# Projections as four column tiles, a merged diagonal step and sums behind the values in an fp32 attention kernel

## Chip, cores and metric

One core of a Trainium2 chip. The time is that of one execution on the device in microseconds; each kernel was executed several times, in rounds beside the kernel before on the same chip. A ratio is the mean time of one kernel's fast runs over that of the other's fast runs of the same rounds, so it is not quite the ratio of the medians quoted beside it. e1 to e4 ran on one chip, e5 to e8 on a second and e9 to e11 on a third; over the rounds the median of the kernel before lay between 2330.8 and 2335.1 us, so differences of a few microseconds between kernels of different groups should not be read.

## The reference

```python
# x: (32, 256, 32, 32) fp32; 8 heads of 32 channels; S = 1024 positions
xn   = group_norm(x, groups=32)                     # groups of 8 channels
q    = q_w @ xn + q_b ;  k, v = split(kv_w @ xn + kv_b)
s    = q k^T / sqrt(32), strictly below the diagonal only (query > key)
out  = x + softmax(s) v                             # position 0 attends to nothing
```

## The kernel before

Everything is fp32, and each fp32 matmul runs as two passes (the trace has eight records for the four matmuls of one step's scores). A *row tile* is a matmul that uses 32 of the 128 rows of TensorE's array, a *column tile* one that uses 32 of its 128 columns; four of them stand side by side. Each way of dividing the array is a *mode* below. PSUM is the memory that TensorE writes to, in banks; a bank is *evacuated* when another engine has read the result out of it. One batch element ("batch" below) is two groups `g` of four heads; each group has two halves `hf` of 512 queries, and each half goes through its blocks `k` of 128 keys. A *step* is one (g, hf, k): 24 a batch. At each step TensorE computes the scores of four heads, ScalarE their exponentials, GpSimd zeroes the triangle of a diagonal block; two steps later (`LAG`) TensorE multiplies with the values, and VectorE adds the exponentials up. In between stand pieces of the next batches: twelve projections a batch, four sums over keys, and two small products for the statistics.

Projections, sums and statistics share **one PSUM bank** (`misc`, `bufs=1`), which the next user gets only when the one before has been evacuated.

```python
ps_s = tc.alloc_tile_pool(name="ps_s", bufs=3, space=PSUM)   # scores, 2 banks each
ps_o = tc.alloc_tile_pool(name="ps_o", bufs=1, space=PSUM)   # acc
ps_m = tc.alloc_tile_pool(name="ps_m", bufs=1, space=PSUM)   # the one bank
def misc(name):
    return ps_m.tile([P, HALF], F32, tag="misc", name=name)

def norm_rstd(b):                                   # statistics, second product
    pv = misc(f"pv_{b}")
    nc.tensor.matmul(pv[:, :NG], lhsT=avg, rhs=live.pop(("dev", b)), start=True, stop=True)
    rstd = small.tile([P, NG], F32, tag="rstd", name=f"rstd_{b}")
    nc.vector.tensor_scalar_add(rstd, pv[:, :NG], 1e-5)
    ...
def project_v(b, n):
    pp = misc(f"ppv_{b}_{n}")...
    # 2 x 2 matmuls of 128x128 by 256 columns
    nc.vector.tensor_add(live["v", b][...], pp, v_bias...)     # evacuated by VectorE
# project_qk: the same with 512 columns, evacuated by ScalarE

def scores(b, g, hf, k):                            # four row tiles (K = 32)
    for j in range(4):
        nc.tensor.matmul(pairs[j // 2][:, j % 2, c0:], lhsT=kk[rows_j, k * P : (k + 1) * P],
                         rhs=q[rows_j, hf * HALF + c0 : (hf + 1) * HALF], start=True, stop=True)
    ...
def values(b, g, hf, k):                            # four column tiles (M = 32)
    for j in range(4):
        nc.tensor.matmul(acc[HD * j : HD * (j + 1), c0:], lhsT=live["v", b][:, k, ...],
                         rhs=e[:, j, c0:], start=k == 0, stop=k == last, skip_group_check=True)
    if k:
        nc.vector.tensor_add(total[:, :, c0:], total[:, :, c0:], e[:, :, c0:])
...
for n, f in zip((4, 6, 10, 14, 16, 18), prepare(b + 2)):      # statistics, normalisation
    when(b * N + n, f)
for n, f in enumerate(projections(b + 1)):
    when(b * N + 2 * n + 1, f)
# main loop: scores(step i); whatever is planned at i; values(step i - LAG)
```

## Time and profile before

| | before |
|---|---|
| time, median | 2332.0 us (2330.8 to 2335.8) |
| busy TensorE / VectorE / ScalarE / GpSimd | 96% / 74% / 59% / 43% |
| period of one batch (start of one `pm` product to the next) | 70.7 us |
| granted TensorE clock (share of the full clock, mean) | 0.994 |

The period is the number to watch: 32 batches of it make up nearly all the time. The prediction below shows the lines of this profile and how they are read.

### The profile page before, as it was taken

Reading aid. Unit: us, or ns where it says so; the run is one execution under the profiler, and the core shown is the slowest. Engines: PE = TensorE matmul, PEld = TensorE weight load, DVE = VectorE, ACT = ScalarE, POOL = GpSimd, SP = SyncE. Lnnn points to the kernel's source line nnn. Section 1 sums busy time; section 2 is a strip of 40 time slices with the busy share of each in tenths; the row PEclk is TensorE's granted clock in tenths of the full one; section 3 lists DMA queues with packets and bytes.
Section 4 is the critical chain, followed back from the end, with each engine's and each line's share of the span. In section 5 each row is a group of like instructions: output and inputs, shape, how many; then the busy total and the mean of one; then the engine's idle time right before and its main releaser. Section 6 shows DMA issues by size and latency. Waiting matters only on the chain.

```text
span 2334.8 us, 37671 instructions
## 1 busy us (share of the span) xinstructions
PE 2243.6 (96%) x15502; PEld 824.2 (35%) x15502; DVE 1735.7 (74%) x1641; ACT 1386.2 (59%) x1921; POOL 1001.5 (43%) x817
## 2 busy tenths in 40 slices
PE   5999999999999999999999999999999999999995
PEld 2333333333333333333333333333333333333331
DVE  2477787877787777787777778777878777877777
ACT  0566666566566566566666665665665665665663
POOL 0234443534543434544434544344435345434346
PEclk9999999999999999999999999999999999999997
DMA  2001111011111011111011111111110111110001
GB/s 88 1 19 55 37 55 55 28 46 42 50 55 55 28 46 37 55 55 55 19 55 37 55 55 38 36 51 41 55 55 28 46 37 55 55 55 28 28 37 55
DMA packets 38033, 104.06 MB, mean 45 GB/s; under 512 B 4192, under 2 KB 5088, under 8 KB 37856
## 3 DMA queue, kind: packets, MB, share of 16 engines
q1 hardware_dynamic: 37856, 101.60, 11.8%
q8 instruction: 123, 2.02, 0.4%
q14 instruction: 54, 0.44, 0.1%
HBM read 34.47 MB, written 33.55 MB: 29 GB/s over the span
## 4 chain that ended last, share of the span: by engine, by line
PE 87%; DVE 8%; issue 2%; ACT 2%; POOL 1%; DMA 0%; SPq 0%; POOLq 0%; DVEq 0%
PE sT L215 27%; PE acc L243 23%; PE pp L176 21%; PE ppv L191 11%; PE pd L260 4%; DVE e L248 3%; DVE xn L163 2%; DVE v L196 1%; DVE den L268 1%; ACT num L252 1%; ACT q L180 1%; POOL e L225 1%; DVE rb L297 0%; PE pv L153 0%; PE pm L141 0%
## 5 line engine op out<-in xcount | busy, mean ns | idle before, releaser
L220 ACT ACTIVATE e<-sT 128x1024 f32<-128x1024 f32 (+3 forms) x1536 | 1148.4, 812 | 668.4 <-PE sT L215 456.3
L248 DVE TENSOR_TENSOR e<-e,e 128x2048 f32<-128x2048 f32 (+3 forms) x640 | 1130.9, 1767 | 221.2 <-PE acc L243 146.9
L225 POOL TENSOR_SCALAR_AFFINE_SELECT e<-e 128x512 f32<-128x512 f32 x512 | 733.3, 1441 | 1284.7 <-ACT e L220 1284.7
L215 PE MATMUL sT<-q,k 32*128 32x512 f32 (+3 forms) x6144 | 811.7, 534 | 0.5 <-ACT e L220 0.5
L243 PE MATMUL acc<-e,v 128*32 128x512 f32 (+3 forms) x6144 | 652.8, 497 | 20.0 <-ACT num L252 11.3
L176 PE MATMUL pp<-xn,wT 128*128 128x512 f32 x1024 | 513.3, 624 | 26.4 <-DVE den L268 20.7
L215 PEld LDWEIGHTS sT<-q,k 32*128 32x128 f32 x6144 | 288.0, 183 | 532.6 <-issue 277.6
L243 PEld LDWEIGHTS acc<-e,v 128*32 128x32 f32 x6144 | 134.9, 108 | 455.1 <-issue 366.3
L176 PEld LDWEIGHTS pp<-xn,wT 128*128 128x128 f32 x1024 | 175.0, 190 | 295.5 <-issue 205.7
L191 PE MATMUL ppv<-wT,xn 128*128 128x256 f32 x1024 | 255.2, 392 | 3.1 <-DVE v L196 2.3
L268 DVE TENSOR_TENSOR den<-den,pd 128x512 f32<-128x512 f32 x96 | 65.6, 684 | 220.2 <-PE pd L260 220.2
L298 POOL TENSOR_TENSOR rb<-rb,x 128x512 f32<-128x512 f32 x128 | 209.2, 1634 | 13.0 <-DVE rb L297 12.6
L191 PEld LDWEIGHTS ppv<-wT,xn 128*128 128x128 f32 x1024 | 184.1, 190 | 66.2 <-issue 33.8
L180 ACT ACTIVATE q<-pp,qk_bias 128x512 f32<-128x512 f32 x128 | 87.9, 687 | 137.4 <-PE pp L176 134.4
L196 DVE TENSOR_TENSOR v<-ppv,v_bias 128x512 f32<-128x512 f32 x128 | 88.3, 690 | 97.3 <-PE ppv L191 97.3
L260 PE MATMUL pd<-e,pick 128*32 128x512 f32 x1024 | 137.2, 608 | 1.2 <-DVE e L248 1.2
L297 DVE TENSOR_TENSOR rb<-num,rb 128x512 f32<-128x512 f32 x128 | 135.3, 1061 | 2.4 <-DMA rb<-rec 2.4
L180 ACT ACTIVATE k<-pp,qk_bias 128x512 f32<-128x512 f32 x128 | 88.1, 688 | 78.2 <-PE pp L176 75.2
L279 DVE RECIPROCAL rec<-den 128x128 f32<-128x128 f32 x128 | 118.7, 931 | 0.0
L252 ACT COPY num<-acc 128x512 f32<-128x512 f32 x128 | 74.2, 580 | 36.5 <-PE acc L243 36.5
L135 DVE BATCH_NORM_STATS2 st<-x 128x6 f32<-128x512 f32 x128 | 80.1, 668 | 4.7 <-DMA x<-in_x_dram 4.7
L163 DVE TENSOR_SCALAR xn<-x,mean,rstd 128x1024 f32<-128x1024 f32 x64 | 68.6, 1074 | 1.6 <-POOL rstd L156 1.6
(40 smaller groups left out, 254.6 us busy)
## 6 DMA issues: line engine op xcount, KB each, us to landing
x<-in_x_dram SPq DMA_DIRECT2D x32, 1024.0 KB, 5.8
rb<-rec SPq DMA_DIRECT2D x128, 256.0 KB, 2.5
out_dram<-rb SPq DMA_DIRECT2D x64, 512.0 KB, 3.0
wn<-in_L_conv_kv_w_dram SPq DMA_DIRECT2D x2, 256.0 KB, 3.4
wn<-in_L_conv_q_w_dram SPq DMA_DIRECT2D x1, 256.0 KB, 2.8
v_bias<-in_L_conv_kv_b_dram SPq DMA_DIRECT2D x1, 128.0 KB, 3.4
qk_bias<-in_L_conv_q_b_dram SPq DMA_DIRECT2D x1, 1.0 KB, 3.4
qk_bias<-in_L_conv_kv_b_dram SPq DMA_DIRECT2D x1, 1.0 KB, 3.1
```

Source lines behind the costliest of these rows:

```text
L176: nc.tensor.matmul(pp, lhsT=wT[:, cc, n * C + g * P : n * C + (g + 1) * P], rhs=live["xn", b][:, cc, cols], start=cc == 0, stop=cc == NG - 1,)
L180: nc.scalar.activation(live[key][:, cols], pp, AF.Identity, bias=qk_bias[:, n, g : g + 1], scale=(SCALE, 1.0)[n],)
L191: nc.tensor.matmul(pp[:, s, :], lhsT=live["xn", b][:, cc, (2 * n + s) * P : (2 * n + s + 1) * P], rhs=wT[:, cc, 2 * C : 3 * C], start=cc = ...
L215: nc.tensor.matmul(pairs[j // 2][:, j % 2, c0:], lhsT=kk[rows, k * P : (k + 1) * P], rhs=q[rows, hf * HALF + c0 : (hf + 1) * HALF], start= ...
L220: nc.scalar.activation(e[:, 2 * a : 2 * a + 2, c0:], pairs[a][:, :, c0:], AF.Exp)
L225: nc.gpsimd.affine_select(out=diagonal, in_=diagonal, pattern=[[0, 4], [1, P]], compare_op=ALU.is_gt, fill=0.0, base=0, channel_multiplier=-1,
L243: nc.tensor.matmul(acc[HD * j : HD * (j + 1), c0:], lhsT=live["v", b][:, k, h * HD : (h + 1) * HD], rhs=e[:, j, c0:], start=k == 0, stop=k ...
L248: nc.vector.tensor_add(total[:, :, c0:], total[:, :, c0:], e[:, :, c0:])
L260: nc.tensor.matmul(pd[HD * j : HD * (j + 1), :], lhsT=pick[:, n, :], rhs=total[:, j, :], start=True, stop=True, skip_group_check=True,)
L279: nc.vector.reciprocal(live["rec", b][:, cols], live["den", b][:, cols])
L297: nc.vector.tensor_mul(rb[:, g, cols], num[:, g, cols], rb[:, g, cols])
L298: nc.gpsimd.tensor_add(rb[:, g, cols], rb[:, g, cols], xt[:, g, cols])
```

## The change

The intent is to take mode changes away from TensorE. Scores use four row tiles, values and sums four column tiles, projections the full array, and each change between these costs time: 0.14 to 0.21 us, as the prediction works out from the trace. Projections are cut into four column tiles, so that they are in the values' mode; the 128-query diagonal block goes into the step of the 384-query one (20 steps a batch instead of 24); sums stand behind the values. The step plan is adapted to 20 steps.

```diff
+        def product(out, lhsT, rhs, start=True, stop=True):
+            for c in range(P // HD):
+                part = slice(HD * c, HD * (c + 1))
+                nc.tensor.matmul(out[part], lhsT=lhsT[:, part], rhs=rhs, start=start, stop=stop, ...)
 # norm_mean, norm_rstd, project_qk, project_v: nc.tensor.matmul(...) -> product(...)
+        def blocks(hf, k):
+            d = k - hf * BPH
+            own = slice(max(d, 0) * P, HALF)
+            if d == 1:
+                return [(k, own, own), (k + 2, slice(0, P), slice(HALF - P, HALF))]
+            return [(k, own, own)]
 # scores, values: a loop over blocks(hf, k) around the four matmuls (and the addition);
 # one exponential and one triangle select for both blocks
-        per = [... for k in range((hf + 1) * BPH)]
+        per = [... for k in range(hf * BPH + 3)]
-                for n, f in zip((4, 6, 10, 14, 16, 18), prepare(b + 2)):
+                for n, f in zip((3, 5, 8, 11, 14, 16), prepare(b + 2)):
-                    when(b * N + 2 * n + 1, f)                       # projections
+                    when(b * N + 1 + n * N // len(units), f)
-                    when(b * N + s + LAG + 2 + (s + LAG) % 2, ... sums)
+                    when(b * N + s + LAG + 1, ... sums, after)       # behind values
-                when(end + BPH + 5 + n, lambda b=b, n=n: finish(b, n))
+                when(end + BPH + 3 + n, lambda b=b, n=n: finish(b, n))
```

More of the change, by code (lines that the diff above doesn't have):

```diff
@@ L123, in misc @@
             return ps_m.tile([P, HALF], F32, tag="misc", name=name)
+        def product(out, lhsT, rhs, start=True, stop=True):
+            for c in range(P // HD):
+                part = slice(HD * c, HD * (c + 1))
+                nc.tensor.matmul(
+                    out[part], lhsT=lhsT[:, part], rhs=rhs, start=start, stop=stop, skip_group_check=True
+                )
         def load(b):
@@ L140, in norm_mean @@
             pm = misc(f"pm_{b}")
-            nc.tensor.matmul(pm[:, :NG], lhsT=avg, rhs=mv[:, :, 0], start=True, stop=True)
+            product(pm[:, :NG], avg, mv[:, :, 0])
             mean = small.tile([P, NG], F32, tag="mean", name=f"mean_{b}")
@@ L152, in norm_rstd @@
             pv = misc(f"pv_{b}")
-            nc.tensor.matmul(pv[:, :NG], lhsT=avg, rhs=live.pop(("dev", b)), start=True, stop=True)
+            product(pv[:, :NG], avg, live.pop(("dev", b)))
             rstd = small.tile([P, NG], F32, tag="rstd", name=f"rstd_{b}")
@@ L175, in project_qk @@
             for cc in range(NG):
-                nc.tensor.matmul(
-                    pp, lhsT=wT[:, cc, n * C + g * P : n * C + (g + 1) * P],
-                    rhs=live["xn", b][:, cc, cols], start=cc == 0, stop=cc == NG - 1,
+                product(
+                    pp, wT[:, cc, n * C + g * P : n * C + (g + 1) * P], live["xn", b][:, cc, cols],
+                    start=cc == 0, stop=cc == NG - 1,
                 )
@@ L190, in project_v @@
                 for cc in range(NG):
-                    nc.tensor.matmul(
-                        pp[:, s, :], lhsT=live["xn", b][:, cc, (2 * n + s) * P : (2 * n + s + 1) * P],
-                        rhs=wT[:, cc, 2 * C : 3 * C], start=cc == 0, stop=cc == NG - 1,
-                        skip_group_check=True,
+                    product(
+                        pp[:, s, :], live["xn", b][:, cc, (2 * n + s) * P : (2 * n + s + 1) * P],
+                        wT[:, cc, 2 * C : 3 * C], start=cc == 0, stop=cc == NG - 1,
                     )
@@ L204, in projections @@
             return units
+        def blocks(hf, k):
[4 more added lines that the diff above has]
+            return [(k, own, own)]
         def scores(b, g, hf, k):
             q, kk = live["q", b, g], live["k", b, g]
-            c0 = max(k * P - hf * HALF, 0)
+            d = k - hf * BPH
             tag = "e0" if k == 0 else "e"
@@ L212, in scores @@
             pairs = [ps_s.tile([P, 2, HALF], F32, tag="sT", name=f"sT_{b}_{g}_{hf}_{k}_{a}") for a in range(2)]
-            for j in range(4):
-                rows = slice(HD * j, HD * (j + 1))
-                nc.tensor.matmul(
-                    pairs[j // 2][:, j % 2, c0:], lhsT=kk[rows, k * P : (k + 1) * P],
-                    rhs=q[rows, hf * HALF + c0 : (hf + 1) * HALF], start=True, stop=True,
-                )
+            for kb, cols, of in blocks(hf, k):
+                for j in range(4):
+                    rows = slice(HD * j, HD * (j + 1))
+                    nc.tensor.matmul(
+                        pairs[j // 2][:, j % 2, cols], lhsT=kk[rows, kb * P : (kb + 1) * P],
+                        rhs=q[rows, hf * HALF + of.start : hf * HALF + of.stop],
+                        start=True, stop=True, skip_group_check=True,
+                    )
+            c0 = 2 * P if d == 2 else 0
             for a in range(2):
                 nc.scalar.activation(e[:, 2 * a : 2 * a + 2, c0:], pairs[a][:, :, c0:], AF.Exp)
-            if k * P >= hf * HALF:
-                diagonal = e[:, :, c0 : c0 + P]
+            if d >= 0:
+                n = 2 if d == 1 else 1
+                diagonal = e[:, :, c0 : c0 + n * P].rearrange("p j (n q) -> p j n q", q=P)
                 nc.gpsimd.affine_select(
-                    out=diagonal, in_=diagonal, pattern=[[0, 4], [1, P]],
+                    out=diagonal, in_=diagonal, pattern=[[0, 4], [0, n], [1, P]],
                     compare_op=ALU.is_gt, fill=0.0, base=0, channel_multiplier=-1,
@@ L233, in values @@
         def values(b, g, hf, k):
-            last = (hf + 1) * BPH - 1
-            c0 = max(k * P - hf * HALF, 0)
+            last = k == hf * BPH + 2
             e = live.pop(("e", b, g, hf, k))
@@ L240, in values @@
             acc, total = live["acc"], live["sum", b, g, hf]
-            for j in range(4):
-                h = 4 * g + j
-                nc.tensor.matmul(
-                    acc[HD * j : HD * (j + 1), c0:], lhsT=live["v", b][:, k, h * HD : (h + 1) * HD],
-                    rhs=e[:, j, c0:], start=k == 0, stop=k == last, skip_group_check=True,
-                )
-            if k:
-                nc.vector.tensor_add(total[:, :, c0:], total[:, :, c0:], e[:, :, c0:])
-            if k == last:
+            for kb, cols, of in blocks(hf, k):
+                for j in range(4):
+                    h = 4 * g + j
+                    nc.tensor.matmul(
+                        acc[HD * j : HD * (j + 1), of], lhsT=live["v", b][:, kb, h * HD : (h + 1) * HD],
+                        rhs=e[:, j, cols], start=k == 0, stop=last, skip_group_check=True,
+                    )
+                if k:
+                    nc.vector.tensor_add(total[:, :, of], total[:, :, of], e[:, :, cols])
+            if last:
                 if (g, hf) == (0, 0):
@@ L302, in finish, with when @@
                 nc.sync.dma_start(out=x_out[b, :, g, :], in_=rb[:, g, :])
-        per = [(g, hf, k) for g in range(NG) for hf in range(NH) for k in range((hf + 1) * BPH)]
+        per = [(g, hf, k) for g in range(NG) for hf in range(NH) for k in range(hf * BPH + 3)]
         steps = [(b, *s) for b in range(B) for s in per]
         N = len(per)
-        at = {}
-        def when(i, f):
-            at.setdefault(i, []).append(f)
+        at, after = {}, {}
+        def when(i, f, where=at):
+            where.setdefault(i, []).append(f)
         def prepare(b):
@@ L321, in unshifted @@
                 when(b * N, lambda b=b: load(b + 2))
-                for n, f in zip((4, 6, 10, 14, 16, 18), prepare(b + 2)):
+                for n, f in zip((3, 5, 8, 11, 14, 16), prepare(b + 2)):
                     when(b * N + n, f)
             if b + 1 < B:
-                for n, f in enumerate(projections(b + 1)):
-                    when(b * N + 2 * n + 1, f)
+                units = projections(b + 1)
+                for n, f in enumerate(units):
+                    when(b * N + 1 + n * N // len(units), f)
             for s, (g, hf, k) in enumerate(per):
-                if k == (hf + 1) * BPH - 1:
-                    when(b * N + s + LAG + 2 + (s + LAG) % 2, lambda b=b, g=g, hf=hf: sums(b, g, hf))
+                if k == hf * BPH + 2:
+                    when(b * N + s + LAG + 1, lambda b=b, g=g, hf=hf: sums(b, g, hf), after)
             end = (b + 1) * N + LAG + 2
@@ L351, in unshifted @@
                     values(*steps[i - LAG])
+                for f in after.get(i, ()):
+                    f()
             worst = const.tile([P, 1], F32, name="worst")
```

## The prediction

> **What bounds the kernel now.** I read first the engine line and the chain of waits on the page, then the groups by shape, then the timeline of TensorE and of VectorE over one steady batch (1000 to 1071 us), then TensorE's own waits and the start and end.
>
> ```profile
> PE 2243.6 (96%) x15502; PEld 824.2 (35%) x15502; DVE 1735.7 (74%) x1641; ACT 1386.2 (59%) x1921; POOL 1001.5 (43%) x817
> PE 87%; DVE 8%; issue 2%; ACT 2%; POOL 1%; DMA 0%; SPq 0%; POOLq 0%; DVEq 0%
> ```
>
> TensorE is busy 96% and is 87% of the chain that ends last. VectorE is second at 74%, and it is already 8% of that chain: it is where a faster TensorE will run into something. How TensorE spends its time shows only in its timeline (columns: start us, us, engine, line, operation, tiles, shape, count):
>
> ```profile
> 1000.23 1.31 PE L215 MATMUL sT<-q,k 32*128 32x512 f32 x8
> 1001.47 1.99 PE L176 MATMUL pp<-xn,wT 128*128 128x512 f32 x4
> 1003.38 1.06 PE L243 MATMUL acc<-e,v 128*32 128x512 f32 x8
> 1004.38 1.14 PE L215 MATMUL sT<-q,k 32*128 32x512 f32 x8
> 1005.45 1.07 PE L260 MATMUL pd<-e,pick 128*32 128x512 f32 x8
> 1006.33 1.04 PE L243 MATMUL acc<-e,v 128*32 128x512 f32 x8
> 1007.30 0.93 PE L215 MATMUL sT<-q,k 32*128 32x384 f32 x8
> ...
> 1021.19 0.42 PE L243 MATMUL acc<-e,v 128*32 128x128 f32 x8
> ...
> 1023.50 0.50 PE L215 MATMUL sT<-q,k 32*128 32x128 f32 x8
> 1023.94 1.99 PE L191 MATMUL ppv<-wT,xn 128*128 128x256 f32 x8
> ```
>
> Ends are modelled, so I take start to next start. A round of 512 columns takes 0.427 us whether it is one full 128x128 matmul or four narrow ones side by side (single matmuls of the trace: pp at 1002.002, 1002.431, 1002.861). What is above that is switching: scores (four row tiles) 1.07 us for two rounds (0.855), so 0.21 over; values (four column tiles) 0.99, so 0.14 over; sums followed by values, both column tiles, 0.88, so only 0.02 over; a projection 1.91 for four rounds (1.71), so 0.20 over. The overheads do not depend on the columns: scores 0.435 at 128, values 0.355 at 128.
>
> Summing these unstalled costs over one batch (two groups; scores 512, 384, 256, 128 and 5x512, 384, 256, 128): scores 20.6, values 18.7, twelve projections 23.0, four sums 3.5, two small statistics products 0.6, together 66.4 us. The measured period is 70.63 us (the same place at 1000.30 and 1070.93 in the chain of waits), so about 4.2 us a batch are waits inside scores for ScalarE's exponentials (a 384-column scores that takes 1.46 instead of 0.86, two 512 ones of 1.84 instead of 1.07) and for VectorE.
>
> **What the Trainium skill says.** "TensorEngine Tiling (Array Packing)", Key Properties: "Changing tiling mode (not just tile) drains the TensorE", and tiles work independently. The trace agrees: 0.02 us over between sums and values, 0.14 to 0.21 us at each change. "SBUF — State Buffer", in the section on its two sides: VectorE with two SBUF inputs and GpSimd lock each other out for a whole instruction. The trace agrees: a triangle select takes 0.63 us alone and 2.4 us beside an addition. "TensorE: Matmul & The Clock Gate", Part 1: after an idle window of some 3.4 us the clock is halved until a busy window. The trace is stricter (windows view: busy us of PE, PEld, DVE, ACT, POOL, then granted clock):
>
> ```profile
> 2288.90:2292.31 3.41, 2.04 (x20) 0.63 (x13) 3.41 (x4) 3.41 (x4) 3.41 (x3) 1.00 0.08 34
> 2292.31:2295.72 3.41, 3.41 (x20) 0.89 (x24) 3.31 (x3) 1.49 (x3) 3.35 (x3) 0.50 0.31 125
> ```
>
> A window with TensorE 60% busy (a gap of 1.37 us) is followed by one at half clock.
>
> **The change part by part.**
>
> Column tiles for projections: a projection becomes 16 (queries, keys) or 32 (values) narrow matmuls in the same number of rounds, four and eight. It now stands in the values' mode, so the change after it goes and the weights of the first round cost 0.03 instead of 0.11: 0.20 us each, 12 a batch, 2.4 us. I take it that four tiles that stream the same xn run as fast as four that stream different e. Issue is no limit: eight 128-column values with their loads need 0.22 us net. The small products: about 0.1 us each, 0.2 us.
>
> Merged diagonal: four steps of 128 columns a batch go. Each cost 0.435 for scores and 0.355 for values, of which 0.43 were rounds that stay; 0.36 us saved each, 1.4 us. ScalarE drops four pairs of exponentials (817 + 381 ns become 1024 ns: 0.17 us each of eight, 1.4 us), which lies off the path, but removes short steps in which it was late. VectorE has the same additions.
>
> Sums behind values: scores-sums-values becomes scores-values-sums, the same number of changes: 0.
>
> Sum on TensorE: 4.0 to 4.2 us a batch, 66.4 to 62.3 us. Going step by step through the 20 new steps, scores plus unit plus values against two exponentials (1.94 us a pair at 512 columns) and evacuations (0.69) and copies (0.58), ScalarE is never more than some 0.1 us late: of the 4.2 us of waits I keep 0.4. So far 62.7 us.
>
> What is given back is on VectorE. There is one bank for projections, sums and statistics; each user waits until the one before is evacuated. Now two such users stand at the same step 11: pv (the variance product) and then, at once, ppv of the third values projection. That one must wait until VectorE has read pv, and VectorE works in order. Before, there were some 1.75 us of TensorE work between, and it was just enough:
>
> ```profile
> 1013.00 0.15 DVE L143 COPY mean<-pm 128x2 f32<-128x2 f32 x1
> ...
> 1016.14 0.68 DVE L196 TENSOR_TENSOR v<-ppv,v_bias 128x512 f32<-128x512 f32 x1
> 1016.74 3.08 DVE L248 TENSOR_TENSOR e<-e,e 128x1536 f32<-128x1536 f32 x2
> 1019.73 1.12 DVE L297 TENSOR_TENSOR rb<-num,rb 128x512 f32<-128x512 f32 x1
> ...
> 1023.71 0.15 DVE L155 TENSOR_SCALAR rstd<-pv 128x2 f32<-128x2 f32 x1
> ```
>
> pv ran at 1022.19, its reader at 1023.71, the next user at 1023.94. In the new order VectorE has between mean and rstd: the 0.94 chain, two additions of 2048 (2.2 and 2.4), one v (0.6), the two of the merged block (1.85 and 0.72), one rb product (1.0): 9.7 us. TensorE has between pm and pv only values 0.99, step 9 3.36, step 10 2.07, scores 1.09 and pm 0.2: 7.7 us. VectorE enters late by 1.5 us (v 0.6, addition 2.2, reciprocal 0.87 after the first ppv, against 2.1 us of TensorE work). So 1.5 + 9.7 - 7.7, plus 0.2 of latency: TensorE stands still for 3.7 us, in every batch that has both (1 to 29; batch 0 has no earlier batch's reciprocals and products, 30 no statistics). The other waits on this bank (the copy of the sums before the next pp, pm before ppv) I put at 0.6 us.
>
> A gap of 3.7 us holds over 1.4 us of at least one 3.41 us window, so the clock halves. Until a full busy window has passed, 3.4 to 6 us of work run at half speed: 1.7 to 3 us lost in the unlucky phases, less if the gap covers the cold window. I take 2.0 us.
>
> Period: 62.7 + 0.6 + 3.7 + 2.0 = 69.0 us, 1.7 below 70.63. Over 29 batches 49 us; batches 0 and 30 without the stall 7 us each; the last batch without projections some 3 us, the start 1 us. 2331 - 67 = 2264 us.
>
> **The rivals.** (a) The stall is small or absent (VectorE less late, or the clock does not drop): the period is 63 to 65 us and the time 2120 to 2190 us. For it: VectorE idles over 16 us a batch today (waits on sums 220 us and on values 147 us in all). Against: those idle spans lie elsewhere in the batch; between mean and rstd there was only 0.45 us. (b) The stall is as I say or longer, and the clock stays low longer: the period is 70.5 to 72 us, 2300 to 2345 us. For it: selects on GpSimd delay additions (2.53 us instead of 2.28 at 1045.38). (c) Column tiles of projections are slower than a full array because four tiles read the same columns: nothing in the trace speaks for it; if each round took 10% more, 2 us a batch, about 65 us in all. (d) GpSimd's merged select (1024 elements) comes too late for the values: two steps later leaves some 5 us after the scores, the select needs some 3 under a lock; unlikely.
>
> **Range and chances.** The gain of 4.1 us and the removed ScalarE waits I hold for firm within 1 us a batch; stall and clock together may be 3 to 8 us. That gives 2190 to 2325 us eight times in ten. Over 2% faster means below 2284 us: 0.63. Slower by over 2% needs over 71.9 us a batch: 0.03. The rest, 0.34, within.
>
> **What would show it.** Right: pp at 1.71 us start to values, values after it with no change; merged scores 1.09; a TensorE wait of 3 to 4 us a batch at ppv, put down to rstd, or to a VectorE instruction; a granted clock of 0.93 to 0.97 in the mean. Wrong: no such wait, clock 1.00 (then rival a), or projections of over 1.8 us at full clock (rival c), or values waiting for the select (rival d).

## The result

| | before | after |
|---|---|---|
| time, median | 2332.0 us (2330.8 to 2335.8) | 2356.6 us (2354.0 to 2359.4) |
| ratio | | 1.0103 |
| period of a batch | 70.7 us | 71.68 us |
| granted clock | 0.994 | 0.951 |

The 95% interval of the ratio is 1.0083 to 1.0123: about 1% slower, within 2%, and outside the predicted range. Page of the changed kernel, engines and chain:

```profile
PE 2113.2 (90%) x22030; PEld 748.7 (32%) x22030; DVE 1732.8 (74%) x1641; ACT 1358.9 (58%) x1665; POOL 722.1 (31%) x689
PE 54%; DVE 40%; issue 5%; ACT 1%; DMA 0%; POOL 0%; SPq 0%; DVEq 0%; POOLq 0%; ACTq 0%
```

TensorE is busy 130 us less, and the time is longer all the same. VectorE does the same work as before, but its share of the chain went from 8% to 40%. TensorE's own waits say where (us in total, times, longest):

```profile
PE ppv L130 <- DVE rstd L164: 143.7, 30, 4.9
PE pd L282 <- DVE e L270: 23.2, 31, 2.6
```

Thirty waits of up to 4.9 us, one a batch, are at the place that the prediction named. TensorE's timeline there:

```profile
1014.00 0.82 PE L234 MATMUL sT<-q,k 32*128 32x256 f32 x8
1015.01 1.93 PE L130 MATMUL ppv<-wT,xn 128*32 128x256 f32 x32 [0.19 <-DVE mean L152]
1016.77 1.04 PE L265 MATMUL acc<-e,v 128*32 128x512 f32 x8
1017.74 1.14 PE L234 MATMUL sT<-q,k 32*128 32x512 f32 x8
1018.81 1.07 PE L265 MATMUL acc<-e,v 128*32 128x384 f32 x16
1019.81 1.31 PE L234 MATMUL sT<-q,k 32*128 32x384 f32 x16
1021.05 0.24 PE L130 MATMUL pv<-dev,avg 128*32 128x2 f32 x8
1026.17 3.64 PE L130 MATMUL ppv<-wT,xn 128*32 128x256 f32 x32 [4.87 <-DVE rstd L164]
1029.58 0.70 PE L265 MATMUL acc<-e,v 128*32 128x256 f32 x8
```

First, the gains are there: `ppv` to the values takes 1.76 us start to start (1015.01 to 1016.77), not 1.92, and the merged scores some 1.1 to 1.2. Then `pv` runs at 1021.05, and the `ppv` that follows it has to wait for VectorE's reading of `pv`, 4.87 us; and when it runs, it takes 3.41 us, twice its time. VectorE meanwhile:

```profile
1014.86 0.09 DVE L152 COPY mean<-pm 128x2 f32<-128x2 f32 x1
1015.00 0.16 DVE L155 TENSOR_TENSOR dev<-mv,mean 128x2 f32<-128x2 f32 x1
1015.19 0.97 DVE L156 TENSOR_TENSOR dev<-dev 128x2 f32<-128x2 f32 x1
1016.20 0.60 DVE L157 TENSOR_TENSOR dev<-dev,mv 128x2 f32<-128x2 f32 x1
1016.72 2.28 DVE L270 TENSOR_TENSOR e<-e,e 128x2048 f32<-128x2048 f32 x1
1018.92 0.68 DVE L204 TENSOR_TENSOR v<-ppv,v_bias 128x512 f32<-128x512 f32 x1
1019.52 5.93 DVE L270 TENSOR_TENSOR e<-e,e 128x2048 f32<-128x2048 f32 x3
1025.37 0.68 DVE L319 TENSOR_TENSOR rb<-num,rb 128x512 f32<-128x512 f32 x1
1025.97 0.14 DVE L164 TENSOR_SCALAR rstd<-pv 128x2 f32<-128x2 f32 x1
```

Between `mean` and `rstd` it is never idle for more than 0.1 us: 11.1 us of work in order, while TensorE had 8.3 us (1013.03 to 1021.29). The last view is the clock (stretches of one clock window each: length, then busy us of PE, PEld, DVE, ACT, POOL, then the granted clock):

```profile
1019.50:1022.90 3.40, 1.80 (x36) 1.39 (x28) 3.30 (x3) 3.26 (x4) 1.51 (x2) 1.00 0.28 103
1022.90:1026.30 3.40, 0.13 (x4) 0.13 (x8) 3.18 (x4) 0.03 (x1) 2.07 (x2) 0.50 0.01 2
1026.30:1029.75 3.45, 3.45 (x36) 1.61 (x39) 0.00 (x0) 0.00 (x0) 1.95 (x3) 0.50 0.00 0
1029.75:1033.20 3.45, 3.45 (x60) 1.54 (x52) 2.77 (x4) 1.67 (x3) 1.08 (x2) 1.00 0.02 5
```

A window in which TensorE was busy 53% is followed by two at half clock (*cold* windows below): one that the wait fills, with TensorE busy 4% of it, and one full of work, which so takes twice as long (3.58 us busy at half clock, 1.8 us lost). It is the second that costs, and it follows a window that was all but idle. This comes once in every batch from the second to the thirtieth, and settles at 71.68 us from one to the next.

### The profile page after: what moved, and what is told of

Read it like the earlier page. It is cut to its first block, busy times and chain, and to the rows that moved or that the text cites. A ratio compares the mean times of both kernels' runs of the same rounds, so it can differ in the third digit from the quotient of the medians.

```text
span 2352.0 us, 49835 instructions
## 1 busy us (share of the span) xinstructions
PE 2113.2 (90%) x22030; PEld 748.7 (32%) x22030; DVE 1732.8 (74%) x1641; ACT 1358.9 (58%) x1665; POOL 722.1 (31%) x689
## 4 chain that ended last, share of the span: by engine, by line
PE 54%; DVE 40%; issue 5%; ACT 1%; DMA 0%; POOL 0%; SPq 0%; DVEq 0%; POOLq 0%; ACTq 0%
DVE e L270 24%; PE pp L130 16%; PE sT L234 12%; PE acc L265 11%; PE ppv L130 10%; PE pd L282 4%; DVE st L144 3%; DVE rec L301 2%; DVE den L290 2%; DVE rb L319 2%; DVE dev L156 1%; DVE xn L172 1%; DVE in_range L295 1%; DVE in_range L294 1%; DVE dev L157 1%
## 5 line engine op out<-in xcount | busy, mean ns | idle before, releaser
L241 ACT ACTIVATE e<-sT 128x1024 f32<-128x1024 f32 (+1 forms) x1280 | 1126.0, 939 | 629.4 <-PE sT L234 532.5
L270 DVE TENSOR_TENSOR e<-e,e 128x2048 f32<-128x2048 f32 (+3 forms) x640 | 1162.7, 1817 | 84.9 <-POOL e L247 48.7
L247 POOL TENSOR_SCALAR_AFFINE_SELECT e<-e 128x512 f32<-128x512 f32 (+1 forms) x384 | 443.3, 1162 | 1464.1 <-ACT e L241 1464.0
L234 PE MATMUL sT<-q,k 32*128 32x512 f32 (+3 forms) x6144 | 710.1, 525 | 0.5 <-ACT e L241 0.5
L130 PE MATMUL pp<-xn,wT 128*32 128x512 f32 x4096 | 494.2, 600 | 13.9 <-DVE den L288 7.8
L130 PE MATMUL ppv<-wT,xn 128*32 128x256 f32 x4096 | 297.1, 439 | 154.2 <-DVE rstd L164 143.7
L265 PEld LDWEIGHTS acc<-e,v 128*32 128x32 f32 x6144 | 176.4, 112 | 391.4 <-issue 309.2
L130 PEld LDWEIGHTS ppv<-wT,xn 128*32 128x32 f32 x4096 | 132.9, 123 | 296.4 <-DVE rstd L164 146.3
L130 PEld LDWEIGHTS pp<-xn,wT 128*32 128x32 f32 x4096 | 107.0, 109 | 318.7 <-issue 201.8
L319 DVE TENSOR_TENSOR rb<-num,rb 128x512 f32<-128x512 f32 x128 | 91.8, 718 | 2.4 <-DMA rb<-rec 2.4
```

What stands on the lines that cost most here:

```text
L130: nc.tensor.matmul(out[part], lhsT=lhsT[:, part], rhs=rhs, start=start, stop=stop, skip_group_check=True)
L234: nc.tensor.matmul(pairs[j // 2][:, j % 2, cols], lhsT=kk[rows, kb * P : (kb + 1) * P], rhs=q[rows, hf * HALF + of.start : hf * HALF + of. ...
L241: nc.scalar.activation(e[:, 2 * a : 2 * a + 2, c0:], pairs[a][:, :, c0:], AF.Exp)
L247: nc.gpsimd.affine_select(out=diagonal, in_=diagonal, pattern=[[0, 4], [0, n], [1, P]], compare_op=ALU.is_gt, fill=0.0, base=0, channel_mu ...
L265: nc.tensor.matmul(acc[HD * j : HD * (j + 1), of], lhsT=live["v", b][:, kb, h * HD : (h + 1) * HD], rhs=e[:, j, cols], start=k == 0, stop= ...
L270: nc.vector.tensor_add(total[:, :, of], total[:, :, of], e[:, :, cols])
```

## The experiments

**Theory A**: the savings on TensorE are real; the wait on the one bank, with VectorE behind, and the halved clock after it take them back. **Rival B**: VectorE is by now the bound of the whole batch, and the wait only shows where. **Rival C**: column tiles cost what they save.

### e4_fill: the same wait, kept busy

```diff
+            for r in range(5 if b >= 2 else 0):
+                product(pv, wT[:, 0, :P], live["xn", b - 1][:, 0, :HALF])
             product(pv[:, :NG], avg, live.pop(("dev", b)))
```

> The changed kernel with the wait kept, but five useless 512-column products (ten rounds, about 4.3 us) put just ahead of the variance product, into the same bank, so that TensorE is busy while VectorE catches up. Theory A (the clock halves because of the gap, and costs about 1.7 us a batch): granted clock back to 0.99, ppv after the wait 1.75 us instead of 3.4, time about 50 us less than the changed kernel, 2290 to 2320 us. If the clock costs nothing, or did not fall because of the gap: 2350 us or more.

Measured: 2305.1 us, ratio 0.987 (0.9854 to 0.9887), 51 us below the changed kernel (54 us by the ratios); clock 0.994; period 69.93 us.

```profile
1003.04 4.50 PE L130 MATMUL pv<-xn,wT 128*32 128x512 f32 x40
1007.35 0.22 PE L130 MATMUL pv<-dev,avg 128*32 128x2 f32 x8
1008.16 1.93 PE L130 MATMUL ppv<-wT,xn 128*32 128x256 f32 x32 [0.58 <-DVE rstd L166]
```

`ppv` still starts as late, but the useless work before it kept the clock up, and it runs at its normal speed. The halved clock costs 71.68 - 69.93 = 1.75 us a batch: a kernel that does more work is faster. The expectation held.

### e1_pv13 and e3_pv13_full: the variance product elsewhere

e1 moves the product away from the projection. e3 is e1 with full-array projections.

```diff
-                for n, f in zip((3, 5, 8, 11, 14, 16), prepare(b + 2)):
+                for n, f in zip((3, 5, 8, 13, 16, 18), prepare(b + 2)):
```

> The changed kernel with the variance product at step 13 instead of 11 (and the two normalisations at 16 and 18), so that no other user of its PSUM bank follows at once. Theory A (the changed kernel's gains are real, and the 4.9 us wait of ppv for rstd plus the halved clock behind it give them back): that wait is gone, granted clock 0.99 or more, period about 64.5 us instead of 71.7, time 2130 to 2180 us. Rival B (VectorE itself is the bound by now, since it is 40% of the chain; taking this wait away moves it to the next sums or values product): 2280 us or more, with new TensorE waits for VectorE of 3 us or more a batch. Rival C (the narrow matmuls cost what they save): about 2260 us, as only stall and clock come back.

> e1_pv13 with the projections as full 128x128 matmuls again (statistics products stay narrow): the merged diagonal, the new step plan and the sums behind values are left. Theory A: 2.0 to 2.4 us a batch more than e1_pv13, some 60 to 75 us, so 2200 to 2250 us, and still 80 us or more below the kernel before. Rival C: the same time as e1_pv13 within 15 us.

Measured: e1 2251.9 us, ratio 0.964 (0.9624 to 0.9656), clock 0.971, period 68.27 us; e3 2256.6 us, ratio 0.9662 (0.9646 to 0.9678), clock 0.985. The wait for `rstd` is gone, but A's numbers were missed by 70 us; e1's time is nearest to the one that C gave. e1's timeline and clock windows:

```profile
1047.10 0.71 PE L234 MATMUL sT<-q,k 32*128 32x256 f32 x8
1050.45 3.52 PE L130 MATMUL ppv<-wT,xn 128*32 128x256 f32 x32 [2.63 <-DVE v L204]
```

```profile
1046.90:1050.30 3.40, 0.92 (x16) 0.31 (x8) 3.37 (x4) 1.67 (x3) 2.17 (x2) 1.00 0.00 0
1050.30:1053.75 3.45, 3.30 (x32) 1.59 (x36) 2.53 (x3) 0.00 (x0) 3.38 (x4) 0.51 0.00 0
```

The next user of the bank now waits, for the evacuation of a values projection by the same late VectorE: 2.6 us a batch, and the clock still halves once a batch. So B is right to this extent: the backlog, not the place of one product, is the cause. e3 looks like a point for C, since full-array projections cost only 5 us more; but in e3 the wait at that place is 1.8 us and the clock falls in 11 batches instead of all. What the column tiles save on TensorE goes there into a longer wait and more cold windows. (e3's batches take 67.8 or 69.1 us, and its 24 batches from 235.26 to 1873.66 us average 68.27 us, e1's period: see the lock under e9.) Whether VectorE is late over the whole batch, or only in a stretch, was open.

### e2_cols_only: the column tiles in the old kernel

```diff
-                nc.tensor.matmul(pp, lhsT=wT[...], rhs=live["xn", b][:, cc, cols], ...)
+                product(pp, wT[...], live["xn", b][:, cc, cols], ...)
 # likewise in project_v; nothing else changed against the kernel before
```

> The kernel before with nothing changed but the twelve projections a batch cut into four column tiles; steps, sums and statistics as before. Theory A: one switch of 0.20 us a projection goes, 2.4 us a batch, 74 us in all: 2250 to 2275 us, start of pp to start of values 1.72 to 1.75 us instead of 1.91, clock 0.99. Rival C (narrow projections are no gain, or ScalarE's waits take it up): 2310 to 2340 us.

Measured: 2281.5 us, ratio 0.9776 (0.976 to 0.9792), period 69.06 us: between the two expectations, 1.6 us a batch instead of 2.4.

```profile
1000.75 1.06 PE L269 MATMUL pd<-e,pick 128*32 128x512 f32 x8
1004.90 1.92 PE L131 MATMUL pp<-xn,wT 128*32 128x512 f32 x16 [0.81 <-DVE den L277]
1006.64 0.40 PE L252 MATMUL acc<-e,v 128*32 128x128 f32 x8
```

`pp` to the values is 1.74 us (1004.90 to 1006.64), as theory A has it, so C is out for the cost on TensorE. Some 0.6 of the missing 0.75 us a batch went into waits that were already there and grew, on `den` (23.6 us in all, 20.7 before) and on ScalarE's copy of the values (16.4 us, 11.3 before), and into new ones on `rstd` (10.5 us).

### e5_spread and e6_spread_full: VectorE's crowded stretch cleared

Nothing is taken from VectorE; its work is moved out of steps 5 to 11. e6 is e5 with full-array projections.

```diff
-                for n, f in zip((3, 5, 8, 11, 14, 16), prepare(b + 2)):
+                for n, f in zip((3, 11, 13, 15, 17, 18), prepare(b + 2)):
                 units = projections(b + 1)
+                units = units[:1] + units[4:8] + units[1:4] + units[8:]   # values projections early
```

> The changed kernel (column tiles, merged diagonal, sums behind values) with VectorE's crowded stretch between steps 5 and 11 cleared: the four values projections, which VectorE evacuates, at steps 2, 4, 6 and 7 instead of 7 to 12, and the second half of the statistics and both small products later (11, 13, 15, applied at 17 and 18). Theory A2 (what gave the gain back is that VectorE works in order and is 3 to 5 us behind in that stretch, so that whichever user of the one bank comes next has to wait, and that a gap of 2.6 us or more halves the clock): no TensorE wait over 1 us left, no cold window in the steady part, period 64 to 65.5 us, time 2130 to 2180 us. Rival B (VectorE is the bound over the whole batch): a new wait of 2 us or more elsewhere, 2230 us or more.

> e5_spread with full 128x128 projections: what the column tiles are worth where no wait hides it. Theory A2: 1.5 to 2.4 us a batch, 45 to 75 us more than e5_spread. Rival C (column tiles are worth nothing): within 15 us of e5_spread, as e3 was of e1.

Measured: e5 **2155.0 us, ratio 0.9244** (0.9229 to 0.926), clock 0.993, no cold window before the last batch, period 64.98 us. e6 2186.7 us, ratio 0.9384 (0.9368 to 0.9399), period 66.01 us. The engines of e5, and its longest wait in the batch:

```profile
PE 2062.7 (96%) x22030; PEld 727.1 (34%) x22030; DVE 1720.4 (80%) x1641; ACT 1355.2 (63%) x1665; POOL 869.6 (40%) x689
```

```profile
PE pd L282 <- DVE e L270: 35.8, 31, 2.6
```

(In a steady batch it is 1.08 us; the 2.6 comes once, in the last batch.) B is out: VectorE does the same work in 65 us as in 72, and is 80% busy. It was late in one stretch. With that cleared, the change that cost 1% is part of a kernel that is 7.6% faster. That is the gain of the change and the new plan together: the new plan was not run in the kernel before, which had some 4.2 us a batch of waits of its own (66.4 against 70.6 us in the prediction). The column tiles are worth 1.03 us a batch here, less than the 1.5 expected: TensorE waits 35.8 us for VectorE ahead of the sums, where e6 waits 13.2, so 0.7 us a batch of what they save is again spent waiting.

### e8_sums_ahead: the order of sums and values

```diff
-                    when(b * N + s + LAG + 1, ... sums, after)
+                    when(b * N + s + LAG + 1, ... sums)          # on e5_spread
```

> e5_spread with the sums ahead of the values in the same step, as the kernel before had them, though one to two steps sooner. On TensorE both orders have the same number of mode changes. Theory: within 0.5% of e5_spread if VectorE has its last addition done by then; where it has not, TensorE waits some 0.9 us longer at each of four sums, up to 3.5 us a batch, 110 us.

Measured: 2224.8 us, ratio 0.9547 (0.9531 to 0.9563), period 67.35 us: 2.4 us a batch more than e5. TensorE's waits:

```profile
PE pd L282 <- DVE e L270: 80.5, 64, 4.0
PE ppv L130 <- DVE den L290: 24.3, 30, 0.8
```

The number of mode changes is the same; the values standing between are the time in which VectorE finishes the last addition. With sums this soon after their half, this part of the change is worth 2.4 us a batch. In the kernel before, sums came one to two steps later, so this is no measure of what the order cost there.

e8 also warns against a simple rule for the clock. Its second sum waits 1.94 us, which leaves windows in which TensorE is busy only 43%, less than in the changed kernel's 53%, and the next window still has the full clock:

```profile
840.55:843.96 3.41, 1.47 (x16) 0.32 (x12) 3.38 (x6) 1.22 (x3) 2.75 (x3) 1.00 0.00 0
843.96:847.38 3.42, 3.42 (x40) 0.97 (x36) 2.27 (x5) 0.62 (x1) 2.79 (x3) 1.00 0.16 67
```

The mean clock of e8 is 0.994. So TensorE's busy share of a window does not by itself decide whether the clock falls; what else does is open.

### e7_rb_later, e9_e1_plus and e10_e5_plus: is the period locked to the clock's windows?

The changed kernel's period is 71.68 us and e1's 68.27 us, batch after batch. From the clock records, one window is 3.4133 us: 21 and 20 windows.

```diff
-                when(end + BPH + 3 + n, lambda b=b, n=n: finish(b, n))    # e7, on the changed kernel
+                when(end + BPH + 7 + n, lambda b=b, n=n: finish(b, n))
+            if n == 2:                        # e9 on e1_pv13, e10 on e5_spread, in sums()
+                product(pd[:, : HALF // 2], wT[:, 0, :P], total[:, 0, : HALF // 2])
```

> The changed kernel with the products of values and reciprocals four steps later (15 to 18 instead of 11 to 14), which takes one VectorE instruction of 0.68 us out of the wait of ppv for rstd. If times simply add, the wait falls from 4.9 to 4.2 us and the time by some 20 us, to 2335 us. Theory L (the period is locked to a whole number of clock windows: the periods measured are 71.68 us = 21 x 3.4133 and, in e1_pv13, 68.27 = 20 x 3.4133, as a gap that begins earlier in a window leaves more work in the cold one): the wait falls by 0.7 us, ppv becomes slower by as much, the period stays 71.68 us and the time within 6 us of the changed kernel's.

> e1_pv13 (period 68.27 us = 20 clock windows, one cold window a batch) with one useless 256-column product, 0.43 us of TensorE work, ahead of the third sum of each batch, where TensorE waits for nothing. Theory L (the period is locked to whole windows): the work begins later in its window, less of it falls into the cold one, and the period stays 68.27 us; time within 4 us of e1_pv13's, ratio to before 0.964. If times add: period 68.70 us, 13 us more, ratio 0.9695.

> The control of e9: the same 0.43 us of useless work at the same place in e5_spread, whose steady part has no cold window. It should be paid in full: period 65.4 us instead of 64.98, 13 us more than e5_spread, ratio to before 0.930 instead of 0.9244. If it is free here too, e9 says nothing on the lock.

Measured: e7 2356.5 us, ratio 1.011 (1.0093 to 1.0127), period 71.68 us. The wait fell to 4.27 us as asked; e7's line, and the window in which `ppv` begins again:

```profile
1030.35 3.64 PE L130 MATMUL ppv<-wT,xn 128*32 128x256 f32 x32 [4.27 <-DVE rstd L164]
1066.94 0.64 PE L265 MATMUL acc<-e,v 128*32 128x256 f32 x8 [0.78 <-POOL e L247]
```

```profile
1028.10:1031.50 3.40, 1.15 (x12) 0.59 (x16) 2.17 (x3) 0.00 (x0) 2.29 (x2) 0.51 0.00 0
```

Work resumed 1.15 us before the end of the first cold window, where it was 0.13 us in the changed kernel, so 1.0 us more of it ran at half clock. e7 is no clean test, as moving the products also brought a new wait of 0.78 us for GpSimd. Still, with the wait for `rstd` 0.60 us shorter, the sum's wait of 0.64 us gone, GpSimd's 0.78 us new and 0.5 us more lost to the clock, the period came out at 71.68 us again.

e9: 2257.8 us, but widely spread (2251.5 to 2267.5), ratio 0.9673 (0.9649 to 0.9697), between the two expectations. Two of the five executions took e1's time (2251.9 and 2251.5), the others 6 to 16 us more. In the profiled one, which is one of the two, the periods go round in fours, 67.39, 68.77, 68.52, 68.39 us: together 273.07 us, 80 windows, 20 a batch as in e1. Its clock records show how: in one batch of four no window is cold (TensorE is busy 49% from 978.10 to 981.51, and the clock stays). The two executions with e1's time have mean clocks of 0.977 and 0.980, the other three 0.970 to 0.974. So the added work was paid for by cold windows that did not come, which is not quite theory L's way (less work in each cold window). e10, the control: 2166.1 us, ratio 0.9276 (0.9264 to 0.9289), period 65.41 us, the full 0.43 us a batch, and no spread (2165.3 to 2168.1); in all 11 us more than e5 on another chip, 7 us by the ratios, where 13 were expected. So the useless work was free in some executions of e9 and never in e10. I take the lock as shown in its effect (exact multiples of the window in four kernels' traces, and e9's free work), and its mechanism (work that resumes earlier in a cold window loses more) as supported by e7, not proved; e9 shows that a batch can also skip its cold window.

### e11_spread2: a further try

e5 with `zip((3, 12, 13, 15, 17, 18), ...)` and `finish` one step later.

> e5_spread with the second half of the statistics at step 12 instead of 11 and the products of values and reciprocals one step later, which takes some 2 us of VectorE work from ahead of the addition that the second sum waits for (1.1 us of TensorE wait a batch in e5). Expected: that wait goes, 0.5 to 1.1 us a batch, 2120 to 2140 us; if GpSimd or VectorE come late elsewhere, the same as e5_spread.

Measured: 2166.2 us, ratio 0.9274 (0.9261 to 0.9286), period 65.40 us: a miss. The wait at the second sum went, and the third sum, which follows `pv` in the bank, now waits 1.56 us for `rstd`. e5_spread stays the fastest kernel found.

## Why the prediction was wrong

The mechanism was right, at the place named: TensorE stands still ahead of the `ppv` that follows `pv`, and the clock halves. The step that failed is the sum "Period: 62.7 + 0.6 + 3.7 + 2.0 = 69.0 us", measured 71.68, in three of its terms: the stall (3.7, measured 4.87), TensorE's own work (62.7, measured 63.9) and the other waits (0.6, measured 1.1).

- **"TensorE stands still for 3.7 us"**: it was 4.87 us. In the terms of "1.5 + 9.7 - 7.7, plus 0.2", VectorE came 1.8 us late (1013.03 to 1014.86) and had 11.1 us of work, and TensorE had 8.3 us. VectorE's 1.4 us more come from two places. The chain after `mean` took 1.86 us instead of 0.94, as its multiplication and its addition of two columns took 0.97 and 0.60 us instead of 0.16 each. The two additions of the merged block took 3.47 us instead of 2.57. (One `rb` product was 0.4 us shorter.) Selects of GpSimd run beside both:

```profile
1015.05 1.10 POOL L247 TENSOR_SCALAR_AFFINE_SELECT e<-e 128x1024 f32<-128x1024 f32 x1 [3.12 <-ACT e L241]
1016.10 0.68 POOL L247 TENSOR_SCALAR_AFFINE_SELECT e<-e 128x512 f32<-128x512 f32 x1
1023.00 1.91 POOL L247 TENSOR_SCALAR_AFFINE_SELECT e<-e 128x1024 f32<-128x1024 f32 x1 [0.51 <-ACT e L241]
1023.98 1.47 DVE L270 TENSOR_TENSOR e<-e,e 128x512 f32<-128x512 f32 x1
```

  The multiplication (1015.19 to 1016.16) ends with the first select (1016.15). In the 29 batches in which a select overlaps it, it takes 0.97 us; in the other three, and in all of the kernel before and of e5, where none does, 0.16. So GpSimd holds VectorE up there; for the merged additions this is read from the one stretch, and no run tests either alone. The prediction named the effect under rival (b), "selects on GpSimd delay additions", with 0.25 us, and its sum had little of it.
- **"So far 62.7 us"**: e4's period less its waits and its fill gives the measured term: 69.93 - 0.58 - 0.64 - 0.27 - 0.19 - 4.31 = 63.9 us. Of the 1.2 us, a projection's 1.74 us instead of 1.71 makes 0.4. That is a slip of the prediction's own: it keeps 0.03 us for the first weights and yet takes off the whole 0.20, and the times that it quotes give 0.429 to 0.430 us for a round, not 0.427. Scores that take 1.24 us instead of 1.07 to 1.09 at four places (1019.81 to 1021.05 is one) make 0.6; the rest is in smaller ones of the same kind.
- **"The other waits on this bank ... 0.6 us"**: 0.19 for `mean`, 0.27 for `den` and 0.64 ahead of the third sum, which was not counted, are 1.1 us.
- **"I take 2.0 us" for the clock**: 1.75 us (e4). That the clock would halve was right, but the ground for it, one window of the profile before at 60% busy, is weaker than it looked: e8's windows at 43% kept the clock. The prediction also took the loss for independent of the rest, which the lock speaks against.
- The sum of the measured terms: 63.9 + 4.87 + 1.1 + 1.75 = 71.6 us against 71.68. So against 69.0 the misses are 1.2, 1.2 and 0.5 us, less 0.25.
- **"The gain of 4.1 us and the removed ScalarE waits I hold for firm within 1 us a batch; stall and clock together may be 3 to 8 us"**: the first half was missed by 0.2 us (63.9 is 1.2 above 62.7), the second held (6.6 us). The range ended at 2325 us, though the sum of its own limits, 63.7 + 0.6 + 8 = 72.3 us, is 2360 us by its count of 29 batches, which covers the measured 2356.6. (By the same count, 2% slower begins at 72.9 us a batch, not 71.9.) Rival (b) gave 70.5 to 72 us a batch and 2300 to 2345 us: its period came true, as did its longer stall, but not its longer loss to the clock, and the time lay 11 us above it.
- **"Sums behind values ... 0"**: right for TensorE's mode changes, wrong for the waits; in e5's plan the order is worth 2.4 us a batch (e8).
- **Column tiles, "2.4 us"**: on TensorE it was some 2.0 us (1.74 to 1.76 us start to start instead of 1.91, twelve times), what came of it in time was 1.6 us a batch in e2, 1.0 in e5 against e6.
- **Merged diagonal, "1.4 us"**: no run has it alone, so its share is not shown.
- Rivals (c) and (d) did not come true in the changed kernel: no projection over 1.8 us at full clock, and 4.2 us in all of values waiting for the select.

## What to carry to other kernels

When TensorE is made faster, add up the in-order work of the evacuating engine between two users of a shared PSUM bank and hold it against the new, shorter TensorE time there: an engine with a 74% mean load was 5 us late in one stretch here, and moving its work by a few steps took the changed kernel from 1% slower to 7.6% faster. Count in what GpSimd does to that engine (0.97 us instead of 0.16 beside a select). A wait can be paid twice: after waits of 1.8 to 4.9 us on TensorE the clock halved in several of these kernels, and the work behind took twice as long. It does not always (e8), so read the granted clock by windows. Where such a wait comes once in a period, the period may snap to whole windows and hide small gains and losses. Put the consumer's slack (here the values) ahead of the instruction that waits, also where the order looks neutral.

## What the Trainium skill lacked or had wrong

- "TensorE: Matmul & The Clock Gate", Part 1, has the clock halved after an idle window of some 3.4 us. Here it was also halved after windows in which TensorE was busy 53% (a gap that had lasted 1.6 us at the window's end) and 60% (a gap of 1.37 us), but not after windows of 43% in e8 (a gap of 1.94 us) and 49% in e9. How idle a window must be stays open.
- The same section says that the window runs free and shifts a kernel's start-up from run to run. It lacks that a periodic kernel can lock to it: periods of 71.68 and 68.27 us are 21 and 20 windows of 3.4133 us, and 0.43 us of added work a batch was free in two of five executions of e9, and paid in full in the control's period.
- "TensorEngine Tiling (Array Packing)", Key Properties, says that a change of tiling mode drains, without a figure: here 0.14 to 0.21 us over the rounds themselves for a group that changes it, 0.02 us for one that stays in its mode.
- The same page, When to Use Tiling, names column tiling for narrow operands (64 columns or fewer). A full 128-column fp32 product cut into four tiles took 1.74 us from its start to that of the values instead of 1.91, where the values that follow are in that mode. That it is the mode alone that saves the 0.17 us is argued, not shown.
